# Mixture of experts with 32 experts: the odd ends of two experts in one tile of rows, and the product moved inside SBUF

## The chip, the core and the metric

The kernel runs on one core of a Trainium2 chip. The metric is the device time of one execution in microseconds (us). Engines are named as in the profile: PE is TensorE's matrix multiplication and PEld its weight loads, DVE is VectorE, ACT is ScalarE, POOL is GpSimd, SP is SyncE, which here only issues transfers. "SPq", "ACTq" and "POOLq" are the instruction queues of these engines where they issue transfers or wait. SBUF is the memory on the core (128 partitions), PSUM the accumulator that PE writes, DRAM the large memory.

## What is computed

One decoder layer in float32 on x of 32 x 128 rows of 512: causal differential attention, cross attention with rotary positions, then a mixture of experts, each with a layer norm ahead and a residual. The change is in the last part:

```python
x = hidden_states.reshape(-1, H)                 # 4096 rows of 512
scores = jax.nn.sigmoid(x @ gate_w)              # 32 experts
# two of four groups of experts, then the best TOP_K = 6 experts of each row
sel_flat = selected_experts.ravel()              # 24576 pairs of row and expert
...
g = jax.lax.ragged_dot(xs, w_gate, group_sizes)  # rows sorted by expert; M = 352
u = jax.lax.ragged_dot(xs, w_up, group_sizes)
d = jax.lax.ragged_dot(jax.nn.silu(g) * u, w_down, group_sizes)
...
expert_out = jnp.sum(out * weights[..., None], axis=1)
shared = jax.nn.silu(x @ sw_gate) * (x @ sw_up) @ sw_down
return (expert_out + shared).reshape(B, S, H)
```

How many rows an expert gets depends on the data. Each expert has 2112 KB of weights (w_gate and w_up 704 KB each, w_down 704 KB).

## The kernel before

Self attention comes first, then cross attention with the routing beside it. The class `Routing` writes each pair of row and expert into a table in DRAM (`table_d`), in which every expert has a region of 128 x 32 slots. The shared expert (`Shared.group`) is computed for eight groups of four blocks of rows: three of them (`EARLY = 3`) ahead of the experts, five behind them. Inside the early groups `between()` is called at fixed places and runs the next step of a list `todo`, which brings the routing to its end and prepares the experts.

**Tiles.** `Routing.tiles` (L1036) cuts each expert's region into tiles of 128 rows: an expert with n rows has ceil(n / 128) of them, and the last one is filled in part. `usual` = 4096 x 6 / 128 + 32 / 2 = 208 tiles are always computed, whether used or not; a second loop behind `tc.If(many > usual)` computes the rest, up to 223, if the data need more. `eid` gives each tile's expert, `fresh` whether its weights must be loaded, `rows` its part of the table. Tiles are dealt out in turn to four sets of weights (`SETS = 4`), and each set goes through 52 tiles in the order of the experts, so most tiles find their weights in place. The weights come from SP (`weights_in` L1379, `weights_out` L1400); a load that isn't needed is skipped by its condition.

**Preparation of the tables.** `fetch` (L1309) gathers the tables with POOL, `arrange` and `turn_tables` sort and transpose them on DVE and PE, `places` (L1357) makes from them, for all tiles, the weights (`weight`), the rows to gather (`run_of`) and the rows to add to (`into`). `first_tokens` starts the first three tiles.

**A tile i** goes through these steps, which `run` (L1508) puts in a fixed order on PE, DVE, ACT and POOL (`manual_schedule`):

- `tokens` (L1416): POOL gathers the tile's rows in four indirect transfers (L1422), 128 rows of 512 bytes each, into `e_xr` (three buffers);
- `turn_in`: DVE transposes them (L1434) to `e_xT`;
- `gate_up` (L1439): PE multiplies by `wg` and `wu` (L1447; each float32 matmul shows as two records), ACT takes silu (L1451), DVE multiplies (L1452) into `e_gu`, of which there is one buffer; ACT issues the write of the product to DRAM (L1454);
- `part_out` (L1459): ACT issues the read back from DRAM (L1463) into `e_gr`, with other rows on the partitions, when the write has landed;
- `turn_out`: two transposes on DVE (L1473) to `e_guT`;
- `down` (L1478): PE multiplies by `wd` (L1483), ACT scales into `e_y` (L1487), POOL adds the rows to `sum_d` in DRAM with an indirect transfer that accumulates (L1488).

In iteration i the order is: gate_up(i), turn_in(i+2), turn_out(i-1), weights_in(i+4), down(i-2), weights_out(i+2), part_out(i), tokens(i+5). So POOL's queue holds, in each iteration, the scatter of tile i-2 and then the four gathers of tile i+5.

Behind the experts the five remaining shared groups run, with the same buffers (`s_pool`) as ahead of them, which stay reserved during the experts' loop.

Of the kernel before, what the change touches and what calls it, by code (L numbers as in the profile page):

```python
# [18 lines left out]
P = 128  # L19
# [867 lines left out]
class Routing:  # L887
# [148 lines left out]
    def tiles(self, eid, fresh, rows, used, usual):  # L1036
# [54 lines left out]
        nc.vector.tensor_scalar(n_i, n, float(P - 1), None, ALU.add)  # L1091
        nc.vector.tensor_scalar(n_i, n_i, 7, None, ALU.logical_shift_right)
        nc.vector.tensor_copy(n, n_i)
        end = tile("end", [P, NX])
# [29 lines left out]
        nc.vector.tensor_tensor(fresh, other, first, ALU.max)  # L1124

# [139 lines left out]
class Experts:  # L1265
# [14 lines left out]
    def __init__(  # L1280
        self, cm, ctx, table_ds, h3_d, sum_d, w_gate, w_up, w_down, eid, fresh, rows, n_tiles
    ):
        self.cm, self.h3_d, self.sum_d, self.eid, self.fresh = cm, h3_d, sum_d, eid, fresh
# [9 lines left out]
        self.dram = ctx.enter_context(tc.tile_pool(name="e_dram", bufs=4, space=DRAM))  # L1293
# [7 lines left out]
        self.gu_s = cp.tile([P, self.Q * self.RUN], F32, name="e_gu")  # L1301

# [4 lines left out]
        self.xr, self.xT, self.gu, self.gr, self.guT = {}, {}, {}, {}, {}  # L1307

    def fetch(self):  # L1309
# [17 lines left out]
        nc.gpsimd.memset(self.gu_s, 0.0)  # L1327
# [29 lines left out]
    def places(self):  # L1357

        nc, cp, T, n_tiles = self.cm.nc, self.cp, self.T, self.n_tiles
        entry = self.entry_ps.rearrange("p o j t -> p o (j t)")[:, :, 0:n_tiles]  # L1360
        self.weight = cp.tile([P, n_tiles], F32, name="e_weight")
        nc.vector.tensor_copy(self.weight, entry[:, 1, :])
# [3 lines left out]
        nc.vector.tensor_copy(row, row_i)  # L1366

        self.run_of = cp.tile([P, self.Q, self.NT * P], I32, name="e_run_of")
        nc.vector.tensor_scalar(
            self.run_of, self.parts_ps.rearrange("p t j x -> p t (j x)"), float(self.Q),  # L1370
            float(-self.Q), ALU.mult, ALU.add,
        )
        nc.vector.tensor_scalar(self.run_of, self.run_of, 0.0, row[:, 1:2], ALU.max, ALU.add)
        none = cp.tile([P, n_tiles], F32, name="e_none")
        nc.vector.tensor_scalar(none, entry[:, 0, :], 0.0, row[:, 0:1], ALU.is_equal, ALU.mult)
        self.into = cp.tile([P, n_tiles], I32, name="e_into")
        nc.vector.scalar_tensor_tensor(self.into, entry[:, 0, :], -1.0, none, ALU.add, ALU.add)

    def weights_in(self, i):  # L1379

        if i >= self.end:
            return
# [17 lines left out]
    def weights_out(self, i):  # L1400

        if i >= self.end:
            return
# [12 lines left out]
    def tokens(self, i):  # L1416

        if i >= self.end:
            return
# [10 lines left out]
    def turn_in(self, i):  # L1430
        if i >= self.end:
            return
# [6 lines left out]
    def gate_up(self, i):  # L1439
        if i >= self.end:  # L1440
            return
        nc = self.cm.nc
        pgu = self.cm.banks()
        t, s = self.xT.pop(i), i % SETS
        for half, w in enumerate((self.wg[s], self.wu[s])):
            for c in range(EC):
                nc.tensor.matmul(  # L1447
                    pgu[:, half, 0:M], t[:, c, :], w[:, c, :], start=c == 0, stop=c == EC - 1
                )
        act = self.p2.tile([P, M], F32, name="e_act", bufs=1)  # L1450
        nc.scalar.activation(act, pgu[:, 0, 0:M], AF.Silu)  # L1451
        nc.vector.tensor_tensor(self.gu_s[:, 0:M], act, pgu[:, 1, 0:M], ALU.mult)  # L1452
        self.gu[i] = self.dram.tile([self.Q, P, self.RUN], F32, name="e_gu_d")
        nc.scalar.dma_start(  # L1454
            out=self.gu[i].rearrange("q s m -> s q m"),
            in_=self.gu_s.rearrange("s (q m) -> s q m", q=self.Q),
        )

    def part_out(self, i):  # L1459


        gr = self.gr[i] = self.p2.tile([P, self.Q, self.RUN], F32, name="e_gr")
        self.cm.nc.scalar.dma_start(  # L1463
# [67 lines left out]
def decoder_kernel(  # L1531
# [90 lines left out]
    with tc.manual_schedule(engines=in_order):  # L1622
# [17 lines left out]
        while todo:  # L1640
            between()
# [68 lines left out]
```

## Time and profile before

| | |
|---|---|
| median of 3 runs | 3912.97 us (3909.75 to 3914.64) |
| the profiled execution's own time | 3913.15 us |
| its span | 3911.4 us |
| busy in the span: PE, PEld, DVE, ACT, POOL | 3793.0, 2015.6, 2057.6, 1678.9, 2349.5 us |
| granted TensorE clock | 0.989 of full speed |
| experts' stage, first L1447 to the first L1215 behind it | 2024.05 to 3618.70 us |
| transfers in the span, by queue (POOL, SP, ACT) | 109.85, 190.98, 82.60 MB |

How to read it: a line of the groups gives source line, engine, operation, what is written and read, tile shape and count, then busy time in us and the mean of one in ns, then the engine's idle time just before these instructions with what ended it ("issue": nothing that the profile shows, the engine's own sequencer). A line of a timeline gives start in us, duration in us, engine, line, operation and count, and in brackets the idle time before. Indirect transfers show on POOL with the time in which POOL makes their descriptors; the transfer itself goes on behind that. Matmul ends are modelled, so intervals between starts are more exact than durations.

### The profile page before, as it was taken

To read this page: it belongs to the slowest core of one execution; us is meant where nothing else is said; L and a number is where in the kernel's file an instruction comes from. 1 tells how busy PE (TensorE), PEld (TensorE's weight loads), DVE (VectorE), ACT (ScalarE), POOL (GpSimd) and SP (SyncE) were. 2 spreads that over 40 slices of the span, in tenths; PEclk is the share of its full clock that TensorE was granted. 3 is DMA by queue.
4 is the path that set the end of the run, shared out by engine and by line. 5 is a ranking of instruction groups with operands and counts; after the bars stand their busy time and mean duration, and the time that the engine had idled before them with its cause. 6 is when DMAs were issued, how large, how long until landed. Compare 5 with 4: busy or idle time off the path is not lost. (4 is left out here: it accounts for less than half of the span.)

```text
span 3911.4 us, 58185 instructions
## 1 busy us (share of the span) xinstructions
PE 3793.0 (97%) x19060; PEld 2015.6 (52%) x19060; DVE 2057.6 (53%) x3202; ACT 1678.9 (43%) x4032; POOL 2349.5 (60%) x2582
## 2 busy tenths in 40 slices
PE   8999999899999999999999999999999999999999
PEld 5666666434444444444445555555555555555444
DVE  5888888777877877776133333333333333332111
ACT  6989999757766776666101111111111111111000
POOL 3545545636777777775347777777777777775000
PEclk9999999899999999999999999999999999999999
DMA  3111110121111111111167777767667676766210
GB/s 110 34 34 38 37 34 27 43 87 57 53 60 47 47 47 47 49 47 50 52 178 168 164 166 170 174 151 174 160 153 167 161 170 147 181 151 150 80 64 32
DMA packets 285987, 387.21 MB, mean 99 GB/s; under 512 B 147888, under 2 KB 179248, under 8 KB 285616
## 3 DMA queue, kind: packets, MB, share of 16 engines
q0 software_dynamic: 62912, 109.85, 15.7%
q1 hardware_dynamic: 81792, 190.98, 15.4%
q10 hardware_dynamic: 140976, 82.60, 7.5%
q8 instruction: 154, 2.52, 0.3%
q14 instruction: 153, 1.25, 0.1%
HBM read 617.52 MB, written 143.07 MB: 194 GB/s over the span
## 5 line engine op out<-in xcount | busy, mean ns | idle before, releaser
L1422 POOL DMA_INDIRECT e_xr<-h_d,e_run_of x832 | 849.2, 1021 | 282.1 <-issue 268.1
L695 DVE TENSOR_REDUCE nm<-ps 128x2 f32<-128x1024 f32 x512 | 611.2, 1216 | 112.1 <-PE ps L691 105.3
L1452 DVE TENSOR_TENSOR e_gu<-e_act,ps 128x352 f32<-128x352 f32 x208 | 108.4, 521 | 974.4 <-ACT e_act L1451 548.8
L718 ACT ACTIVATE xp<-ps 128x1024 f32<-128x1024 f32 x512 | 505.9, 1021 | 265.0 <-PE ps L691 200.9
L1483 PE MATMUL ps<-wd,e_guT 128*128 128x512 f32 (+1 forms) x1248 | 585.2, 605 | 34.6 <-ACT e_y L1487 15.7
L714 PE MATMUL ps<-xqn,xk 32*128 32x512 f32 x2048 | 527.1, 620 | 20.6 <-ACT xp L718 19.2
L1447 PE MATMUL ps<-wu,e_xT 128*128 128x352 f32 x1664 | 528.6, 461 | 7.4 <-DMA wu<-in_L_ffn_w_up_dram 5.1
L1447 PE MATMUL ps<-wg,e_xT 128*128 128x352 f32 x1664 | 527.9, 460 | 5.3 <-DMA wg<-in_L_ffn_w_gate_dram 4.5
L691 PE MATMUL ps<-xk,xq 32*128 32x512 f32 x2048 | 526.9, 630 | 0.5 <-DVE nm L695 0.4
L1451 ACT ACTIVATE e_act<-ps 128x352 f32<-128x352 f32 x208 | 96.5, 464 | 935.2 <-PE ps L1447 443.7
L1488 POOL DMA_INDIRECT sum_d<-e_y,e_into x208 | 335.8, 1615 | 178.1 <-ACT e_y L1487 91.6
L1447 PEld LDWEIGHTS ps<-wg,e_xT 128*128 128x128 f32 x1664 | 315.1, 190 | 243.2 <-issue 108.8
L1447 PEld LDWEIGHTS ps<-wu,e_xT 128*128 128x128 f32 x1664 | 316.4, 191 | 186.6 <-DMA wu<-in_L_ffn_w_up_dram 8.3
L279 ACT ACTIVATE s<-s,a_nm 128x128 f32<-128x128 f32 x1024 | 395.7, 396 | 4.9 <-DVE a_nm L265 4.5
L1483 PEld LDWEIGHTS ps<-wd,e_guT 128*128 128x128 f32 (+1 forms) x1248 | 239.8, 194 | 291.7 <-issue 226.5
L1487 ACT ACTIVATE e_y<-ps,e_weight 128x512 f32<-128x512 f32 x208 | 143.0, 687 | 431.3 <-PE ps L1483 265.0
L714 PEld LDWEIGHTS ps<-xqn,xk 32*128 32x128 f32 x2048 | 168.6, 183 | 284.3 <-ACT xp L718 123.3
L1473 DVE STREAM_TRANSPOSE e_guT<-e_gr 96x384 f32<-96x384 f32 (+1 forms) x416 | 230.5, 554 | 76.2 <-DMA e_gr<-e_gu_d 53.5
L228 POOL TENSOR_SCALAR k<-kz,a_keep,a_extra 128x256 f32<-128x256 f32 x128 | 82.6, 655 | 287.4 <-ACT kz L227 287.4
L1028 POOL DMA_INDIRECT table_d<-entry,at x192 | 202.1, 1053 | 64.7 <-issue 53.2
L729 PE MATMUL ps<-xp,v 128*32 128x512 f32 x2048 | 233.0, 595 | 7.9 <-ACT xp L718 7.6
L1434 DVE STREAM_TRANSPOSE e_xT<-e_xr 128x512 f32<-128x512 f32 x208 | 226.3, 1088 | 8.8 <-DMA e_xr<-h_d,e_run_of 8.8
(272 smaller groups left out, 5282.6 us busy)
## 6 DMA issues: line engine op xcount, KB each, us to landing
wg<-in_L_ffn_w_gate_dram SPq DMA_DIRECT2D x208, 704.0 KB
wu<-in_L_ffn_w_up_dram SPq DMA_DIRECT2D x208, 704.0 KB
wd<-in_L_ffn_w_down_dram SPq DMA_DIRECT2D x208, 576.0 KB
e_gu_d<-e_gu ACTq DMA_DIRECT2D x208, 192.0 KB
e_gr<-e_gu_d ACTq DMA_DIRECT2D x208, 192.0 KB
wd<-in_L_ffn_w_down_dram SPq DMA_DIRECT2D x208, 128.0 KB
e_xr<-h_d,e_run_of POOLq DMA_INDIRECT x832
xres<-in_x_dram SPq DMA_DIRECT2D x32, 256.0 KB
```

The source lines that it names most:

```text
L279: nc.scalar.activation(s[:, j, c, side, :], s[:, j, c, side, :], AF.Exp, bias=nm[n][:, side, at : at + 1], accum_out=sm[n][:, to : to + 1],)
L691: self.nc.tensor.matmul(sc[:, i, :], q[rows, ts(c, P)], k[rows, :], start=True, stop=True)
L695: self.nc.vector.tensor_reduce(at[:, self.ROW[side], 2 * pair : 2 * pair + 2], sc, AX.X, ALU.max, negate=True)
L714: self.nc.tensor.matmul(sc[:, i, :], k[rows, ts(c, P)], q[rows, :], start=True, stop=True)
L718: self.nc.scalar.activation(e, sc, AF.Exp)
L729: self.nc.tensor.matmul(po[b, side][ts(j, 32), :], self.v2[b % 2][:, c, 2 * j + side, :], es[j // 2][:, j % 2, :], start=c == 0, stop=c == ...
L1422: self.cm.nc.gpsimd.indirect_dma_start(out=xr[:, t, :], out_offset=None, in_=self.h3_d.rearrange("t (q f) -> (t q) f", q=self.Q), in_offse ...
L1434: self.cm.nc.vector.transpose(xT.rearrange("p c (t i) -> p c t i", t=self.Q), self.xr.pop(i).rearrange("p t (j c) -> p c t j", c=EC),)
L1447: nc.tensor.matmul(pgu[:, half, 0:M], t[:, c, :], w[:, c, :], start=c == 0, stop=c == EC - 1)
L1473: self.cm.nc.vector.transpose(t[rows, 0:n, :].rearrange("p c (t i) -> p c t i", t=self.Q), g[rows, :, 0 : 32 * n].rearrange("p t (j c) -> ...
L1483: nc.tensor.matmul(py, t[:n, c, :], self.wd[s][:n, c, :], start=c == 0, stop=c == len(M_CHUNKS) - 1)
L1488: nc.gpsimd.indirect_dma_start(out=self.sum_d[:, :], out_offset=bass.IndirectOffsetOnAxis(ap=self.into[:, i : i + 1], axis=0), in_=y[:, :] ...
```

## The change

There are now 192 whole tiles (`usual`) and 8 shared ones (`mixed`). `Routing.tiles` counts each expert's rows in units of 64. If that number is odd, the last 64 slots are an odd end; the first 16 odd ends go two by two into shared tiles, and further ones get a tile of their own as before. The threshold of the second loop is now 192 of 223 tiles.

- `Routing.halves` (new) works out on DVE, by comparing and summing, which expert and which rows of the table belong to each of the 16 ends.
- `fetch_halves`, `arrange_halves`, `turn_halves`, `places_of_halves`, `mixed_places` (new) do for the ends what the steps above do for tiles. They stand in `todo` behind `first_tokens`: four table gathers on POOL, sorting on DVE, six small transposes on PE in the last early shared group, and small DVE instructions.
- `mixed_loads` (new): the weights of the two experts of a shared tile don't come from SP but are gathered by POOL, row by row: ten indirect transfers for each shared tile, four with rows of 5632 bytes (704 KB each) and six with rows of 2048 bytes. One is issued at the end of each of the first ten iterations, and again of the ten iterations behind each shared tile. There is one buffer for each of the two experts (`xg`, `xu`, `xd`).
- `seq` places shared tile m at position 25 m + 14 of 200.
- In a shared tile, PE multiplies the lower 64 columns by one expert's weights and the upper 64 by the other's, alternately, into the two halves of the same PSUM tile.
- A shared tile is added to `sum_d` in two scatters, one for each half; in each, the other half's rows go to unused rows. Both halves may hold the same row of x.
- The product stays in SBUF: `part_out` and the DRAM buffers are gone, there are two `e_gu` buffers, and ACT issues four transfers of 48 KB (eight of 24 KB in a shared tile) from `e_gu` to `e_gr`.
- `e_gu`, `e_gr`, the scaled result (`e_out`, four buffers, before `e_y` with two) and the shared tiles' weights lie in a pool of their own, made in the room of the shared groups' buffers and of cross attention's; the shared groups' buffers are made again behind the experts.

The diff, cut to its core:

```diff
@@ Routing.tiles
-        nc.vector.tensor_scalar(n_i, n, float(P - 1), None, ALU.add)
-        nc.vector.tensor_scalar(n_i, n_i, 7, None, ALU.logical_shift_right)
+        nc.vector.tensor_scalar(n_i, n, float(P // 2 - 1), None, ALU.add)
+        nc.vector.tensor_scalar(n_i, n_i, 6, None, ALU.logical_shift_right)
+        odd_i = tile("odd_i", [P, NX], I32)
+        nc.vector.tensor_scalar(odd_i, n_i, 1, None, ALU.bitwise_and)
...
+        nc.vector.tensor_scalar(alone, nth, float(2 * mixed), None, ALU.is_le)
+        nc.vector.tensor_tensor(odd, odd, alone, ALU.mult)
+        nc.vector.tensor_tensor(n, n, odd, ALU.subtract)
@@ Experts
+    def mixed_loads(self):
+        top = (self.Q - 1) * 32
+        rows = [w.rearrange("e (p c) m -> (e p) (c m)", p=P) for w in self.w_in]
+        out = self.w_out.rearrange("e k m -> (e k) m")
+        for m in range(self.mixed):
+            work = [
+                (x[h].rearrange("p c m -> p (c m)"), src, P, 0, h)
+                for x, src in zip((self.xg, self.xu), rows) for h in range(2)
+            ] + [
+                (self.xd[h][:, c, :], out, top if c == 2 else P, 1 + c, h)
+                for c in range(len(M_CHUNKS)) for h in range(2)
+            ]
+            for to, src, n, at, h in work:
+                k = 2 * m + h
+                self.cm.nc.gpsimd.indirect_dma_start(
+                    out=to[0:n],
+                    out_offset=None,
+                    in_=src,
+                    in_offset=bass.IndirectOffsetOnAxis(ap=self.x_rows[0:n, at, k : k + 1], axis=0),
+                    bounds_check=src.shape[0] - 1,
+                )
+                yield
@@ gate_up
+            for half, w in enumerate((self.xg, self.xu)):
+                for c in range(EC):
+                    for h in range(2):
+                        lanes = ts(h, P // 2)
+                        nc.tensor.matmul(
+                            pgu[lanes, half, 0:M], t[:, c, lanes], w[h][:, c, :],
+                            start=c == 0, stop=c == EC - 1,
+                        )
...
-        nc.scalar.dma_start(
-            out=self.gu[i].rearrange("q s m -> s q m"),
-            in_=self.gu_s.rearrange("s (q m) -> s q m", q=self.Q),
-        )
-    def part_out(self, i):
...
+        for q in range(self.Q):
+            to, part = gr[ts(q, 32)], gu[:, ts(q, self.RUN)]
+            if i < self.n_tiles:
+                nc.scalar.dma_start(out=to, in_=part)
+            else:
+                for h in range(2):
+                    nc.scalar.dma_start(out=to[:, ts(h, 2), :], in_=part[ts(h, P // 2)])
@@ down
+        for into in [self.into[:, i : i + 1]] if m < 0 else [self.into_half[:, h, m : m + 1] for h in range(2)]:
+            nc.gpsimd.indirect_dma_start(
+                out=self.sum_d[:, :],
+                out_offset=bass.IndirectOffsetOnAxis(ap=into, axis=0),
...
+                compute_op=ALU.add,
+            )
@@ run
+            for k in range(len(seq) + 2):
+                each(self.gate_up, k)
+                each(self.turn_in, k + 2)
+                each(self.turn_out, k - 1)
+                each(lambda i: self.weights_in(i + SETS), k)
+                each(self.down, k - 2)
...
+                each(self.tokens, k + 5)
+                if left:
+                    next(loads, None)
+                    left -= 1
+                if k < len(seq) and seq[k] >= self.n_tiles:
+                    left = 10
@@ decoder_kernel
-    usual = T * TOPK // P + NX // 2
+    usual, mixed = T * TOPK // P, NX // 4
...
             experts.first_tokens,
+            experts.fetch_halves,
+            nothing,
+            nothing,
+            experts.arrange_halves,
+            experts.turn_halves,
+            experts.places_of_halves,
+            experts.mixed_places,
         ]
...
+    x_out.close()
+    e_out = ExitStack()
+    experts.rooms(e_out.enter_context(tc.tile_pool(name="e_p3", bufs=1, reuse_waits="tile")))
     experts.run()
```

## The prediction

> **What bounds the kernel now.** I read the table of busy time by stage first, because the change touches one stage only, the expert stage. Columns: stretch in us, its length, then busy us and count of PE, PEld, DVE, ACT and POOL, the granted clock, the DMA share and GB/s.
>
> ```profile
> 2024.00:3619.00 1595.00, 1546.26 (x4579) 871.61 (x4578) 535.94 (x831) 238.96 (x416) 1163.24 (x1019) 0.99 0.69 162
> ```
>
> PE is busy for 97% of the stage and POOL for 73%, so PE looks like the only bound. The groups of POOL's instructions in the same stage correct this: each indirect transfer has idle time in front of it that ends by "issue", that is, by nothing but POOL's own sequencer.
>
> ```profile
> L1422 POOL DMA_INDIRECT e_xr<-h_d,e_run_of x812 | 828.9, 1021 | 255.6 <-issue 241.9 <-DVE e_xT L1434 10.0 <-DVE e_gu L1452 3.4
> L1488 POOL DMA_INDIRECT sum_d<-e_y,e_into x208 | 335.8, 1615 | 178.1 <-ACT e_y L1487 91.6 <-issue 72.9 <-DMA sum_d<-e_y,e_into 13.5
> ```
>
> The timelines of the two engines over the same 10 us show what that means for a tile (start, duration, instruction):
>
> ```profile
> 2065.78 1.61 POOL L1488 DMA_INDIRECT sum_d<-e_y,e_into  x1 [0.30 <-issue]
> 2067.70 1.06 POOL L1422 DMA_INDIRECT e_xr<-h_d,e_run_of  x1 [0.30 <-issue]
> 2069.06 1.00 POOL L1422 DMA_INDIRECT e_xr<-h_d,e_run_of  x1 [0.31 <-issue]
> 2070.37 1.01 POOL L1422 DMA_INDIRECT e_xr<-h_d,e_run_of  x1 [0.30 <-issue]
> 2071.68 1.01 POOL L1422 DMA_INDIRECT e_xr<-h_d,e_run_of  x1 [0.30 <-issue]
> 2073.00 1.62 POOL L1488 DMA_INDIRECT sum_d<-e_y,e_into  x1 [0.30 <-issue]
> ```
>
> ```profile
> 2062.87 2.53 PE L1447 MATMUL ps<-wg,e_xT 128*128 128x352 f32 x8
> 2065.24 2.53 PE L1447 MATMUL ps<-wu,e_xT 128*128 128x352 f32 x8
> 2067.61 2.74 PE L1483 MATMUL ps<-wd,e_guT 128*128 128x512 f32 x6
> 2070.18 2.53 PE L1447 MATMUL ps<-wg,e_xT 128*128 128x352 f32 x8
> ```
>
> A tile costs PE 2070.18 - 2062.87 = **7.31 us**, and POOL 2073.00 - 2065.78 = **7.22 us** (four gathers 5.30, one scatter 1.92). POOL is within 1.2% of PE: nothing can be put on it without making it the bound. The stage lasts from 2024.05 (first L1447) to 3618.70 (first L1215 behind it), 1594.65 us. 208 x 7.31 = 1520.5; the other 74 are about 17 for the last tiles' chain and 57 of PE waits, with matmuls at half pace behind a long one:
>
> ```profile
> 3573.17 5.46 PE L1483 MATMUL ps<-wd,e_guT 128*128 128x512 f32 x6 [4.09 <-DVE e_guT L1473]
> ```
>
> (six records took 5.46 us, otherwise 2.74). In that time POOL waited too: from its first gather for the sixth tile (2031.39) to its last (3578.4 + 1.0) are 1548 us, with 203 x 5.30 + 201 x 1.92 = 1462 of work and some 86 of waiting, mostly the 91.6 behind e_y.
>
> **The change, part by part.** *Tiles on PE.* From the reference's inputs the experts receive 673 to 842 rows; in units of 64 rows that makes 191 whole tiles and exactly 16 odd ends. So 192 + 8 tiles do, and the loop for more than 192 is skipped. PE saves 8 x 7.31 = 58.5 us. A shared tile has twice the records, each on 64 columns of the array; two neighbours should run together. No row has 64 columns; 32 columns, four at a time, is the nearest:
>
> ```profile
> 1305.02 3.64 PE L729 MATMUL ps<-xp,v 128*32 128x512 f32 x32 [0.25 <-ACT xp L718]
> 1305.48 0.13 PEld L729 LDWEIGHTS ps<-xp,v 128*32 128x32 f32 x4 [0.30 <-issue]
> 1305.90 0.13 PEld L729 LDWEIGHTS ps<-xp,v 128*32 128x32 f32 x4 [0.30 <-issue]
> ```
>
> Four records go every 0.43 us, the pace of one full one (2.57 us for six of L1483), and their weights load beside them. Each change of array shape costs about 0.2 (L1254's four records fill 1.06 us, 2022.99 to 2024.05, instead of 0.86), four changes per shared tile: 8.1 us each, +6 in all; if nothing overlapped, +58. I take +6: PE work 1468 us. The Trainium skill, "TensorE: Matmul & The Clock Gate", Part 3, speaks against that: a weight load overlaps a running matmul only if its row group differs, and both halves use all 128 rows. L729's loads use the same rows too and start with the matmuls of the round before, so the trace decides; by the rule, with 22 pairs of loads exposed at 0.11 to 0.19 us, a shared tile would take 10 to 11 us as an estimate, some 20 us in all.
>
> *POOL.* From the same point (first gather of the sixth tile) to the last gather there are now:
> - gathers for 195 tiles: 195 x 5.30 = 1033.5;
> - scatters in between: 193 tiles, of which 8 scatter twice: 201 x 1.92 = 386;
> - 80 weight gathers (10 per shared tile). The trace has none with rows of 5632 or 2048 bytes. Gathers of 512-byte rows take 1.01, the table's (L1320) of 1 KB 1.01 to 1.09, scatters of 8 bytes (L1028) 0.97: length does not show. The other end is the accumulating scatter with 2 KB rows, 1.61. With 0.30 in front: 80 x 1.27 = 102 to 80 x 1.91 = 153. I take 80 x 1.31 = 105, the row that also gathers;
> - a wait in each pair of scatters: POOL holds a scatter until the one before has landed (the third releaser of L1488 above). By the trace's landing events a scatter lands 4.9 us after its start (median of 202, longest 9.3), so the second starts 3.0 later than it could. In seven of eight a 704 KB gather is issued just ahead in the same queue (such a load from SP lands in 4.5). I take 4 each, 32; ends 0 and 8 x 7.4 = 59.
>
> Sum 1556.5. Behind the waiting scatter stand the next tile's four gathers, for which DVE and then PE wait.
>
> *Start.* POOL issues the ends' table gathers behind the first 12 token gathers (1997.50 + 12 x 1.31 = 2013.2), 5.2 us with four; they land near 2020, DVE sorts them in about 1.5, and PE's six small transposes, which stand in its order at about 2018.5, wait: +3.5 for all that follows. Ends: 0, and 6 if the 38 small DVE instructions (0.16 to 0.25 each, some 8 us) also make the table transposes at 1987.69 late; the tables were sorted at 1985.5, 2.2 us earlier. The 20 gathers ahead of the loop end 6.4 us later than before, inside POOL's idle 7.87 before 2031.39.
>
> *Product within SBUF.* One hop replaces two, and no instruction on ACT waits any longer for the write to DRAM. ACT issues four transfers for two, 4 x 0.37 instead of 0.71 us, at 239 busy us of 1595. This can remove up to the 57 us of PE waits; I count 0, since POOL is then late instead. The cover gone (POOL cheap), it counts. The Trainium skill, "DMA: Bandwidth & Descriptors", Rules for kernel authors, has transfers under 64 KB as mostly overhead, and these are 48 KB; with the 2.0 us of fixed cost that its section on the anatomy of one DMA gives for GpSimd's path, four one after another would be, as an estimate, 8 us for a tile, over PE's 7.31. No run here shows SBUF to SBUF; the 192 KB reads took 2.4 us to land at the median.
>
> *DMA and the end.* The bounce took 18.3% of the engines' time in the stage (79.5 MB); the weight gathers bring 16 x 2.16 = 35 MB, at the rate of SP's weights (67 MB in 13.5%) 7%. The share falls, so I count 0. At the end s_gu and its pool are laid out again over the experts' tiles; they are needed 7 us into the group, when the last scatter has landed: 0.
>
> *Sum.* Last gather ends at 2031.4 + 3.5 + 1556.5 = 3591.4. Behind it come landing 2.1 (3.1 from its start), transpose 1.1, gate and up 4.7, down of the tile before the last but one 2.6, and two more downs with the last product's way, about 6: 16.5. The shared groups start at 3608 instead of 3618.7: -10.8, and 1.8 I give back for waits that a queue at its limit will meet: -9. The profiled execution took 3913.15 (span 3911.4), 0.2 above the median of the runs, 3912.97. Forecast **3904**.
>
> **The rivals.** *PE stays the bound*: POOL's additions fit in after all. Then start 3.5 + 1468 + 57 + 17 = 1545.5, -49: 3864; 3807 if the waits go too. For it: POOL idled 86 us. Against it: these idle times were PE's stalls, and 105 + 32 us of new work are more. *A weight gather costs what an accumulating scatter costs*: long rows make POOL write more descriptors. Then 80 x 0.60 = 48 more, 3952, slower; it decides from 1.31 + 9/80 = 1.42 us for a gather with its gap. For it: the only 2 KB rows of the trace take 1.61; against it: those accumulate, and 8 to 1024 bytes cost alike. *It does not do what it says*: counts differ on the chip, more than 192 whole tiles, and the second loop runs its 31: +227, 4131.
>
> **How the numbers follow.** POOL the bound at its rows: 0.60, from 3885 (pairs at 2 us, start at 0) to 3922 (pairs at 6, start at 6); of that 0.34 faster, 0.20 within, 0.06 slower. PE the bound 0.10 (faster). Dear gathers 0.27 (slower). Second loop 0.03 (slower). A difference under 0.2% (8 us) can't be told from none. Range 3872 to 3950: it leaves out the second loop, half of "PE the bound" and a third of the dear gathers, 0.17.
>
> **What would show it.** POOL in the expert stage without idle time other than "issue", DVE's e_xT waiting for e_xr, and PE idle before the gate matmuls (L1621 in the changed kernel) for DVE: right. POOL waiting for e_y as now: wrong, PE is the bound. The weight gathers' mean against 1.01, the idle time before the second scatter against 4, a shared tile's PE time against 8.1, the first L1621 against 2028, and the waits of PE for e_guT, which should go, test the terms one by one.

## The result and the profile after

The changed kernel takes 4089.44 us (median of 4 runs, 4063.41 to 4107.61), the kernel before on the same chip 3911.36: a ratio of **1.045 (1.039 to 1.0509)**, slower. The forecast was 3904, the range ended at 3950. The profiled execution of the changed kernel took 4107.61, its span 4105.9.

The expert stage of the changed kernel, in the columns of the table by stage above (stretch, length, busy us and count of PE, PEld, DVE, ACT, POOL, granted clock, DMA share, GB/s):

```profile
2024.00:3830.00 1806.00, 1574.42 (x4618) 854.38 (x4617) 514.74 (x820) 226.85 (x402) 1215.91 (x1072) 0.94 0.61 141
```

The stage begins as before (first L1621 at 2024.2) and now ends at 3809.96 (first L1268; the last 20 us of the stretch are the shared groups'), 191 us later. PE is busy for 87% of it, POOL for 67%: both shares fell (from 97% and 73%), so waiting has grown on both. Its groups show who waits:

```profile
L1599 POOL DMA_INDIRECT e_xr<-h_d,e_run_of x800 | 817.4, 1022 | 271.8 <-issue 229.7
L1664 PE MATMUL ps<-wd,e_guT 128*128 128x512 f32 (+1 forms) x1152 | 600.0, 661 | 220.9 <-issue 144.6
...
L1671 POOL DMA_INDIRECT sum_d<-e_out,e_into x192 | 310.3, 1616 | 259.9 <-ACT e_out L1668 186.8
L1668 ACT ACTIVATE e_out<-ps,e_weight 128x512 f32<-128x512 f32 x200 | 137.4, 687 | 774.9 <-DMA e_gr<-e_gu 300.0
```

800 gathers are 200 tiles, so the second loop did not run. PE stands before `down` for 221 us (34.6 before), POOL before its scatter for 260 us (178 before), mostly for ACT's e_out, as it did for e_y. Two different things lie in this, and one loading iteration shows both. First POOL's timeline in the changed kernel (start, duration, instruction, idle time before):

```profile
2871.16 1.61 POOL L1671 DMA_INDIRECT sum_d<-e_out,e_into  x1 [0.30 <-issue]
2873.07 1.06 POOL L1599 DMA_INDIRECT e_xr<-h_d,e_run_of  x1 [0.30 <-issue]
2874.44 1.01 POOL L1599 DMA_INDIRECT e_xr<-h_d,e_run_of  x1 [0.31 <-issue]
2875.76 1.01 POOL L1599 DMA_INDIRECT e_xr<-h_d,e_run_of  x1 [0.31 <-issue]
2877.07 1.01 POOL L1599 DMA_INDIRECT e_xr<-h_d,e_run_of  x1 [0.30 <-issue]
2878.39 1.01 POOL L1538 DMA_INDIRECT xu<-in_L_ffn_w_up_dram,e_x_rows  x1 [0.30 <-issue]
2879.70 1.61 POOL L1671 DMA_INDIRECT sum_d<-e_out,e_into  x1 [0.30 <-issue]
...
2904.03 1.01 POOL L1538 DMA_INDIRECT xd<-in_L_ffn_w_down_dram,e_x_rows  x1 [0.30 <-issue]
2911.40 1.61 POOL L1671 DMA_INDIRECT sum_d<-e_out,e_into  x1 [6.36 <-ACT e_out L1668]
```

An iteration with a weight gather takes POOL 8.54 us (2871.16 to 2879.70) without any pause, where PE needs 7.31: POOL is the bound there. That I had forecast. The second thing I had not. PE and ACT in the same stretch:

```profile
2876.74 2.53 PE L1621 MATMUL ps<-wu,e_xT 128*128 128x352 f32 x8
2879.11 2.74 PE L1664 MATMUL ps<-wd,e_guT 128*128 128x512 f32 x6
2881.68 2.53 PE L1621 MATMUL ps<-wg,e_xT 128*128 128x352 f32 x8
2884.05 2.53 PE L1621 MATMUL ps<-wu,e_xT 128*128 128x352 f32 x8
2894.06 4.72 PE L1664 MATMUL ps<-wd,e_guT 128*128 128x512 f32 x6 [7.47 <-issue]
```

```profile
2877.04 0.69 ACT L1668 ACTIVATE e_out<-ps,e_weight 128x512 f32<-128x512 f32 x1 [3.23 <-remote]
2890.91 0.46 ACT L1634 ACTIVATE e_act<-ps 128x352 f32<-128x352 f32 x1 [13.19 <-remote]
2891.96 2.52 ACTq L1641 DMA_DIRECT2D e_gr<-e_gu  x4
...
2906.77 0.46 ACT L1634 ACTIVATE e_act<-ps 128x352 f32<-128x352 f32 x1 [10.84 <-remote]
```

PE has done the `wu` matmuls by 2879.3, ACT has been free since 2877.7, and yet the silu that needs nothing else starts at 2890.91, **11.6 us late**. The view names "remote" as its releaser, that is, no instruction that it can tell, and the trace records PE's signal at 2890.83: the signal itself arrived late. DVE's signal to PE does not: `wd` at 2894.06 starts 0.1 us after the transpose that it waits for. This goes on for one more tile, until POOL, out of work, pauses from 2905.04 to 2911.40; 1.7 us into this pause four of PE's signals are recorded within 0.26 us, and ACT goes on at 2906.77. PE has meanwhile waited 7.47 us, and its next six records take 4.72 us instead of 2.74.

The kernel before has it too. ACT's waits for such signals, before and then after (engine, tile, line, releaser: us, times, longest):

```profile
ACT e_act L1451 <- remote: 153.6, 24, 10.8
```

```profile
ACT e_act L1634 <- remote: 296.6, 35, 13.2
```

The 4.09 us of PE's waiting at 3573.17, which I had shown in the prediction, are of this kind, though the view gives "PE" as the releaser: PE's `wu` ended at 3561.8, silu began at 3570.03, 1.2 us after POOL had stopped at 3568.81 (PE, POOL and ACT of the kernel before):

```profile
3559.24 2.53 PE L1447 MATMUL ps<-wu,e_xT 128*128 128x352 f32 x8
3567.80 1.01 POOL L1422 DMA_INDIRECT e_xr<-h_d,e_run_of  x1 [0.30 <-issue]
3570.03 0.46 ACT L1451 ACTIVATE e_act<-ps 128x352 f32<-128x352 f32 x1 [9.51 <-PE ps L1447]
```

### The profile page after: what moved, and what is told of

Same layout as the page of the kernel before. It is cut to its first block, busy times and chain, and to the rows that moved or that the text cites. A ratio compares the mean times of both kernels' runs of the same rounds, so it can differ in the third digit from the quotient of the medians.

```text
span 4105.9 us, 58585 instructions
## 1 busy us (share of the span) xinstructions
PE 3804.0 (93%) x19066; PEld 1989.4 (48%) x19066; DVE 2042.8 (50%) x3231; ACT 1664.8 (41%) x4016; POOL 2402.4 (59%) x2638
## 3 DMA queue, kind: packets, MB, share of 16 engines
q8 instruction: 154, 2.52, 0.3%
## 5 line engine op out<-in xcount | busy, mean ns | idle before, releaser
L1599 POOL DMA_INDIRECT e_xr<-h_d,e_run_of x800 | 817.4, 1022 | 271.8 <-issue 229.7
L1664 PE MATMUL ps<-wd,e_guT 128*128 128x512 f32 (+1 forms) x1152 | 600.0, 661 | 220.9 <-issue 144.6
L1621 PE MATMUL ps<-wg,e_xT 128*128 128x352 f32 x1536 | 488.4, 460 | 3.2 <-DMA wg<-in_L_ffn_w_gate_dram 2.0
L1621 PE MATMUL ps<-wu,e_xT 128*128 128x352 f32 x1536 | 486.9, 459 | 3.1 <-issue 3.0
L1671 POOL DMA_INDIRECT sum_d<-e_out,e_into x192 | 310.3, 1616 | 259.9 <-ACT e_out L1668 186.8
L1668 ACT ACTIVATE e_out<-ps,e_weight 128x512 f32<-128x512 f32 x200 | 137.4, 687 | 774.9 <-DMA e_gr<-e_gu 300.0
L1621 PEld LDWEIGHTS ps<-wg,e_xT 128*128 128x128 f32 x1536 | 292.3, 191 | 230.0 <-issue 105.1
L1621 PEld LDWEIGHTS ps<-wu,e_xT 128*128 128x128 f32 x1536 | 291.7, 190 | 166.0 <-issue 4.0
L1651 DVE STREAM_TRANSPOSE e_guT<-e_gr 96x384 f32<-96x384 f32 (+1 forms) x400 | 219.5, 549 | 46.1 <-DMA e_gr<-e_gu 26.6
L1609 DVE STREAM_TRANSPOSE e_xT<-e_xr 128x512 f32<-128x512 f32 x200 | 217.3, 1086 | 35.6 <-DMA e_xr<-h_d,e_run_of 35.5
```

Of the source, the lines that this page charges most:

```text
L1599: self.cm.nc.gpsimd.indirect_dma_start(out=xr[:, t, :], out_offset=None, in_=self.h3_d.rearrange("t (q f) -> (t q) f", q=self.Q), in_offse ...
L1609: self.cm.nc.vector.transpose(xT.rearrange("p c (t i) -> p c t i", t=self.Q), self.xr.pop(i).rearrange("p t (j c) -> p c t j", c=EC),)
L1621: nc.tensor.matmul(pgu[:, half, 0:M], t[:, c, :], w[:, c, :], start=c == 0, stop=c == EC - 1)
L1651: self.cm.nc.vector.transpose(t[rows, 0:n, :].rearrange("p c (t i) -> p c t i", t=self.Q), g[rows, :, 0 : 32 * n].rearrange("p t (j c) -> ...
L1664: nc.tensor.matmul(py[lanes], t[:n, c, lanes], wd[:n, c, :], start=c == 0, stop=c == last)
L1671: nc.gpsimd.indirect_dma_start(out=self.sum_d[:, :], out_offset=bass.IndirectOffsetOnAxis(ap=into, axis=0), in_=y[:, :], in_offset=None, b ...
```

## The experiments

My theory after this result: POOL is the bound where it gathers weights, and on top of it PE's signals come late while POOL issues without pause. Rivals: the transfers within SBUF slow ACT or the loads; the weight gathers cost by the traffic they bring, not by POOL's time; the pair of scatters is the price.

The chips differ. The kernel before takes 3911 to 3914 us where the result and e1 to e4 were taken, and 3854 on the three chips of all other runs, so each ratio is against the kernel before on the same chip.

| run | us | before | ratio (95%) |
|---|---|---|---|
| e1_loads_once | 3978.46 | 3913.71 | 1.0148 (1.011 to 1.0187) |
| e2_dram_path | 4041.17 | 3913.71 | 1.0316 (1.0295 to 1.0336) |
| e3_sbuf_only | 3954.10 | 3913.71 | 1.0092 (1.0071 to 1.0113) |
| e4_gathers_only | 4024.12 | 3913.71 | 1.0274 (1.0249 to 1.0298) |
| e5_sp_loads | 3907.96 | 3853.56 | 1.0146 (1.0126 to 1.0166) |
| e6_act_order | 3855.58 | 3853.56 | 1.0011 (1.0000 to 1.0022) |
| e7_pool_busy | 3944.79 | 3853.56 | 1.0227 (1.021 to 1.0244) |
| e8_three_gathers | 3855.04 | 3853.56 | 1.0004 (0.9995 to 1.0014) |
| e9_after | 3946.50 | 3853.94 | 1.0244 (1.0224 to 1.0263) |
| e3b_sbuf_only | 3855.29 | 3853.94 | 1.0009 (0.9998 to 1.0019) |
| e10_sp_loads_order | 3885.50 | 3853.94 | 1.0078 (1.0061 to 1.0095) |
| e11_sp_loads_dram | 3895.94 | 3853.94 | 1.0102 (1.0084 to 1.012) |
| e4b_gathers_only | 3964.77 | 3853.86 | 1.0291 (1.0273 to 1.0308) |
| e12_one_load | 3844.35 | 3853.86 | 0.9975 (0.9966 to 0.9985) |
| e13_spread | 3881.13 | 3853.86 | 1.0075 (1.0058 to 1.0093) |
| e14_one_scatter | 3811.76 | 3853.86 | 0.9887 (0.9871 to 0.9904) |
| e15_late_scatter_dram | 3881.76 | 3854.40 | 1.0074 (1.0059 to 1.0088) |
| e16_late_scatter_sbuf | 3869.61 | 3854.40 | 1.0043 (1.003 to 1.0057) |

### The parts one by one

**e1_loads_once**: the changed kernel; weights are gathered for the first shared tile alone.

```diff
-        for m in range(self.mixed):
+        for m in range(1):
             work = [
```

> The changed kernel, but POOL gathers the shared tiles' weights only for the first of the eight; the other seven multiply by those of the first, so their rows are wrong and 70 of 80 weight gathers are left out. Theory A (POOL's queue: while POOL makes descriptors for indirect transfers with no pause over 1 us, PE's signals that its matmuls are done reach ACT late; the weight gathers remove POOL's pauses): a tile costs POOL 7.22 us again against PE's 7.31, the late signals fall back to what they are in the kernel before (214 us in sum on ACT against 462), and the time is 3860 to 3910 us. Theory B (the four transfers inside SBUF: 2.5 us of issue on ACT for a tile, and their completion semaphores shared with SP's weight loads): only 70 x 1.31 us can go, 4000 us or more. Theory C (the shared tiles themselves, their matmuls on half the columns and their second scatter): 4000 us or more.

**e2_dram_path**: the changed kernel with the product through DRAM, as before.

```diff
-        for q in range(self.Q):
-            to, part = gr[ts(q, 32)], gu[:, ts(q, self.RUN)]
...
+        d = self.gu[i] = self.dram.tile([self.Q, P, self.RUN], F32, name="e_gu_d")
+        if i < self.n_tiles:
+            nc.scalar.dma_start(
+                out=d.rearrange("q s m -> s q m"), in_=gu.rearrange("s (q m) -> s q m", q=self.Q)
+            )
...
+                each(self.part_out, k)
                 each(self.tokens, k + 5)
```

> The changed kernel with the product by way of DRAM as before (one write and one read on ACT for a tile, eight writes and one read for a shared tile). Theory A (weight gathers keep POOL without pauses): little changes, 4050 to 4110 us. Theory B (four transfers inside SBUF): back to 3905 to 3930 us. Theory C (shared tiles): as A.

**e3_sbuf_only**: 208 whole tiles as before, the product within SBUF. **e4_gathers_only**: 208 whole tiles, the product through DRAM, and the 80 weight gathers into buffers that nobody reads.

```diff
-    usual, mixed = T * TOPK // P, NX // 4
+    usual, mixed = T * TOPK // P + NX // 2, NX // 4
...
-            lambda: routing.tiles(eid, fresh, rows, used, usual, mixed),
+            lambda: routing.tiles(eid, fresh, rows, used, usual, 0),
...
-        experts.begin(0, usual, mixed)
+        experts.begin(0, usual)
```

> Only the second half of the change: 208 whole tiles and no shared ones, no weight gathers, the product moved inside SBUF by four transfers. Theory A: POOL has the work of the kernel before, so 3890 to 3915 us. Theory B: the four transfers are the cause and the time is 4000 us or more. Theory C: as A.

> 208 whole tiles with the product by way of DRAM, as in the kernel before, and 80 weight gathers on POOL in eight groups of ten iterations, into buffers that nothing reads. Theory A: 4030 us or more: the ten iterations of each group cost POOL 8.53 us instead of 7.22, and in them PE's signals come late as in the changed kernel. Theories B and C: only POOL's sum counts, 80 x 1.31 = 105 us less the some 86 us that POOL waits in the kernel before, about 3932 us.

Against the kernel before, the changed kernel has +178 us, e1 +65, e2 +127, e3 +40, e4 +110. The gathers are worth some 110 by both ways of asking: e1 leaves 70 of the 80 out (178 - 65 = 113), e4 adds them. The way within SBUF costs 40 by itself and 178 - 127 = 51 in the changed kernel, where I had counted nothing or a gain. e1, e2 and e3 each fall between the ranges set for the theories, so no single theory is the whole cause; e4 comes 6 us under what the first one asked for.

### What a gather costs by

**e7_pool_busy**: e4 with a POOL instruction of about the same length, without traffic, in place of each weight gather. **e8_three_gathers**: whole tiles through DRAM with three of four token gathers; DVE copies the third quarter for the fourth. **e5_sp_loads**: the changed kernel, the shared tiles' weights loaded by SP. **e6_act_order**: e3 with ACT's four transfers behind the e_out of the same iteration.

```diff
@@ e7
-                self.cm.nc.gpsimd.indirect_dma_start(
...
+                self.cm.nc.gpsimd.memset(self.xg[0].rearrange("p c m -> p (c m)")[:, 0:1408], 0.0)
@@ e8
-        for t in range(self.Q):
+        for t in range(self.Q - 1):
...
+        nc.vector.tensor_copy(xr[:, 3, :], xr[:, 2, :])
@@ e5
+                for to, src in zip((self.xg[h], self.xu[h]), self.w_in):
+                    e = expert(2 * m + h)
+                    self.last = nc.sync.dma_start(
+                        out=to, in_=src[ds(e, 1)].rearrange("o (p c) m -> p (o c) m", p=P)
+                    )
+                    yield
@@ e6
                 each(self.down, k - 2)
+                each(self.part_out, k)
```

> The changed kernel, but SP loads the shared tiles' weights (eight plain transfers for each tile, spread over six iterations) and POOL gathers none. Theory A (the weight gathers cost by POOL's queue): as the run in which they were left out, or a little less, 3955 to 3985 us, though as many bytes move. Rival A' (the 35 MB of weights cost by the DMA engines, whoever issues them): 4050 us or more.

> 208 whole tiles with the product moved inside SBUF, as in the run that took 3954 us, but ACT issues the four transfers of tile k behind e_out of tile k-2 and not ahead of it. Theory A, second part (each time that POOL runs dry, it waits until ACT has done e_act, issued the transfers, 2.5 us, and done e_out): POOL's pauses become about 2 us shorter and the time falls to 3890 to 3915 us. Rival B' (the transfers cost by the semaphores that they share with SP's weight loads, or by their own number): 3945 us or more.

> 208 whole tiles with the product by way of DRAM, as in the run with 80 weight gathers that nothing reads (4024 us), but each of these gathers is replaced by a memset of 128x1408 on POOL, which should take about 1.2 us like a gather with its gap. Theory A, first part (it is the making of descriptors without a pause that holds PE's signals back): the memsets are pauses in it, the signals come in time, and the time is 3945 us or less. Rival A'' (any work that fills POOL does the same, since POOL's own chain of scatter and gathers is the bound in these iterations): 4005 to 4035 us.

> 208 whole tiles with the product by way of DRAM, as in the kernel before, but POOL gathers only three quarters of each tile's rows (the fourth is a copy of the third on DVE, so the experts' output is wrong): POOL has 5.9 us of work for a tile and pauses in each. Theory A: PE's signals come in time and the 57 us of PE's waits go: 3850 to 3865 us. Rival (the late signals have another cause, PE's own queue or the weight loads): 3900 us or more.

The group of POOL's added instructions in e7:

```profile
L1540 POOL MEMSET xg<- 128x1408 f32 x80 | 103.3, 1291 | 0.0
```

103 us of POOL's time without a byte moved cost 91. **A gather costs mostly by POOL's time**: on such a chip the real gathers, 80 x 1.31 = 105 us of it, cost 111 (e4b below). The 20 us between the two can be traffic, for PE's waits for weights are 20.8 us in e4b and 6.8 in e7; they were not taken apart. But e8 gives POOL 1.31 us less in each tile and gains nothing: in the kernel before, on this chip, PE alone is the bound. POOL at 7.22 beside PE's 7.31 is harmless; at 8.54 nearly all of the excess counts. With the weights by SP (e5) POOL is relieved, 38 us quicker than the changed kernel on such a chip (e9 below), but PE now waits for whole tiles' weights: 40.5 us for `wd` and 27.9 for `wg`. e6's order changes nothing here (3855.58; e3b, without it, 3855.29).

This chip's kernel before was 60 us quicker than the first one's, and no ACT row with "remote" was in these traces. The expectations of these four stand in the first chip's times; without late signals e6, e7 and e8 do not test what they say of such signals. So the changed kernel itself had to be run on such a chip.

### The changed kernel on another chip

**e9_after** is the changed kernel, unchanged; **e3b_sbuf_only** repeats e3. **e10_sp_loads_order** is e5 with e6's order, **e11_sp_loads_dram** e5 with the product through DRAM.

```diff
@@ e10: e5, and
                 each(self.down, k - 2)
+                each(self.part_out, k)
@@ e11: e5, and
+        nc.scalar.dma_start(
+            out=d.rearrange("q s m -> s q m"), in_=gu.rearrange("s (q m) -> s q m", q=self.Q)
+        )
```

> The changed kernel itself, beside the kernel before on the same chip, because the kernel before took 3913 us on one chip and 3854 us on another, where PE's signals were never late. If PE's late signals make most of the loss, the changed kernel loses little on a chip without them (under 2%); if POOL's queue and SP's late weight loads make it, it loses 3 to 4.5% on any chip.

> 208 whole tiles with the product moved inside SBUF, transfers ahead of e_out, once more, beside the kernel before on the same chip. If the transfers' 2.5 us on ACT cost only by making the pauses longer that follow PE's late signals: within 0.3% of the kernel before on a chip without late signals, 1% slower on one with them. If they cost by themselves: 1% slower on any chip.

> Shared tiles with their weights loaded by SP, and the four (eight) transfers inside SBUF issued behind e_out. In the run with SP's loads and the old order (1.0146 of before), PE waited 80 us for wg and wd, whose loads SP issued late: it waited 270 us in front of wg and wu for product transfers that shared their completion semaphores. That theory (eight semaphores for eight transfers in an iteration): still 1.01 or more of before. Rival (what is late is e_out, and by it POOL and all that follows): below before, 0.99.

> Shared tiles with their weights loaded by SP, and the product by way of DRAM as before (one write, one read; two reads in a shared tile), so that an iteration uses six completion semaphores and not eight. Theory of the semaphores: SP is no longer late, the 8 x 7.31 - 6 = 52 us of PE come through for the most part, 0.988 to 0.993 of before. Rival (a shared tile's second scatter and its other steps cost what it saves): 1.00 or more.

The same program takes 3946.5 here and 4089.4 there: 143 us that go with the chip, and all of them lie in the experts' stage (the first L1621 stands at 2024.2 there and 2024.4 here, and behind the stage come 296 and 294 us). The ratio of e9 lies between its two forecasts, under 2% and 3 to 4.5%. Of the way within SBUF nothing is left (e3b 1.0009). e10 and e11 stay over the kernel before: PE waits 37.1 us for `wg` and 16.6 for `wd` in e10; 25.2, 16.7 and 14.4 for `wg`, `wu` and `wd` in e11. e11 speaks against the theory that completion semaphores (the signals that a transfer has landed) shared by too many transfers make the weights late: it forecast 0.988 to 0.993. e10 fits neither of its two. A loading iteration of e9, PE and then ACT:

```profile
2592.53 2.53 PE L1621 MATMUL ps<-wu,e_xT 128*128 128x352 f32 x8
2594.90 2.74 PE L1664 MATMUL ps<-wd,e_guT 128*128 128x512 f32 x6
```

```profile
2591.53 0.69 ACT L1668 ACTIVATE e_out<-ps,e_weight 128x512 f32<-128x512 f32 x1 [3.23 <-DMA e_gr<-e_gu]
2595.16 0.46 ACT L1634 ACTIVATE e_act<-ps 128x352 f32<-128x352 f32 x1 [2.94 <-PE ps L1621]
2596.21 2.52 ACTq L1641 DMA_DIRECT2D e_gr<-e_gu  x4
```

Silu starts 0.1 us after the last `wu` record, with POOL as busy as on the other chip. I summed, for each trace, the time by which silu and e_out started over 0.9 us after ACT was free and PE's modelled end was past: 214 us in the kernel before, 462 after, 314 in e1, some 390 to 400 in e2, 306 in e3, 410 in e4; on the chips where the kernel before takes 3854, not one such event. Where there are such events, they gather in stretches in which POOL issues with no pause over 0.9 us. In the kernel before 32 such stretches, 18 to 51 us long, hold all 78 events: 55 of the late starts come while POOL still issues, the other 23 at most 1.2 us into its next pause. In the changed kernel the stretches are 7 to 68 us long and the pause reaches 1.8 us. On the other chips POOL runs 135 us (e9) and 217 us (e4b) without a pause and nothing comes late.

### The rest of the price

**e4b_gathers_only** repeats e4 here. **e12_one_load**: e11, the weights loaded for the first shared tile alone. **e13_spread**: e11 with a load in every third iteration. **e14_one_scatter**: e12 with the first of the two scatters alone.

```diff
@@ e12
-        for m in range(self.mixed):
+        for m in range(1):
@@ e13
-                    if left <= 6:
+                    if left % 3 == 0 or k < 14:
                         next(loads, None)
...
-                    left = 8
+                    left = 20
@@ e14
-        for into in [self.into[:, i : i + 1]] if m < 0 else [self.into_half[:, h, m : m + 1] for h in range(2)]:
+        for into in [self.into[:, i : i + 1]] if m < 0 else [self.into_half[:, 0, m : m + 1]]:
```

> 208 whole tiles, product by way of DRAM, 80 weight gathers that nothing reads, once more, beside the kernel before on the same chip. On a chip where PE's signals are not late (before at 3854 us) the same with memsets in place of the gathers took 91 us more than before. If the gathers cost by the time that they take in POOL's order, the same here: 85 to 100 us. If most of their 111 us on the first chip came from late signals: under 60 us.

> Shared tiles, product by way of DRAM, SP loads the shared tiles' weights only for the first of the eight (the others multiply by these, so their rows are wrong). If the 66 us that PE waits for weights in the run with all eight (42 us over before) come from these loads, in SP's queue or on the DMA engines: 0.988 to 0.994 of before. If they come from the order in which SP's other loads stand around a shared tile, or from the second scatter: 1.005 or more.

> As the run with shared tiles, SP's loads and the product by way of DRAM (1.0102 of before), but the loads of a shared tile stand in every third iteration and not in six iterations one after another. If it is their crowding: below 1.000 of before. If it is their number, or another cause: 1.005 or more.

> As the run with SP's loads for the first shared tile only, and each shared tile is added with its first scatter alone (the rows of its second half are left out). If the second scatter's wait (4 us each, 29.7 to 37.5 us in eight, in the traces) is on the path: 25 to 45 us below that run. If POOL's pauses hide it: within 8 us of it.

e4b costs 111, as e4 did (110), where 85 to 100 or under 60 were expected: the gathers' price does not depend on late signals. e11 against e12 is 52 us: seven shared tiles' weights by SP, which then come late; spread out (e13) they still cost 37. e14 against e12 is 33 us: the second scatters, on the path. e12 and e14 are quicker than the kernel before, but only without a part of the work; e14's -42 is what fewer tiles bring when only the first shared tile's loads stand against it.

**e15_late_scatter_dram** and **e16_late_scatter_sbuf** issue the second scatter behind the next tile's gathers, so that it need not wait, on e13 and on e10 with e13's spread loads.

```diff
-        for into in [self.into[:, i : i + 1]] if m < 0 else [self.into_half[:, h, m : m + 1] for h in range(2)]:
...
+            self.add(y, self.into_half[:, 0, m : m + 1])
+            self.later = y, self.into_half[:, 1, m : m + 1]
...
                 each(self.tokens, k + 5)
+                if mixed[1]:
+                    self.add(*self.later)
```

> The version that the runs point to: shared tiles, their weights loaded by SP in every third iteration, the product by way of DRAM, and the second scatter of a shared tile issued behind the next tile's four gathers (5.3 us), by when the first has landed (4.9 us). The run with spread loads took 1.0075 of before, the second scatter's wait 33 us: 3881 - 33 = 3848, 0.997 to 1.000 of before. If the wait only moves to another place: 1.005 or more.

> The same with the product inside SBUF, its transfers issued behind e_out: 79 MB less on the DMA engines, so that the weights land earlier, against eight completion semaphores in an iteration. With six loads crowded it took 1.0078 of before where DRAM took 1.0102. If the DMA engines' load makes the weights late: 0.990 to 0.996 of before. If the semaphores do: 1.000 or more.

POOL's waits before its scatter in e13, then in e15:

```profile
POOL sum_d L1694 <- DMA sum_d<-e_out,e_into: 36.5, 21, 4.1
POOL sum_d L1694 <- DMA sum_d<-e_out,e_into_half: 32.0, 8, 6.3
```

```profile
POOL sum_d L1700 <- DMA sum_d<-e_out,e_into: 50.8, 22, 4.1
...
POOL sum_d L1700 <- DMA sum_d<-e_out,e_into_half: 5.4, 3, 4.2
```

e15 gains nothing (1.0074 against 1.0075). The wait only moved: the eight plain scatters that now stand right behind a late one waited 33.5 us in all, whatever the view names as their releaser, where the pairs of e13 had waited 32.0. e16 is the quickest version with shared tiles and the whole output, still 15 us over the kernel before: none here beats it. Its 1.0043 falls on the side of the semaphores, which e11 spoke against. PE waits 12.2 us for `wg` and `wu` in e16 and 45.7 in e15 (whose profiled execution, 3901 us, is the slowest of its six); the two differ in the product's way and in ACT's order, and what makes the weights late stays open.

## Why the prediction was wrong, point by point

**What failed.** The step "*Product within SBUF* ... This can remove up to the 57 us of PE waits; I count 0, since POOL is then late instead" is the largest miss. I took the 57 us for waits that a later POOL would cover. They were PE's signals coming late on this chip while POOL does not pause, and a late signal holds POOL too: its scatter waits for e_out, 186.8 us in the row L1671 of the profile after (5.8 in e9), for which the sum had nothing. My sign that PE is the bound, POOL waiting for the scaled result, thus showed where neither engine was. Taken as the difference between the chips, the late signals cost 59 us in the kernel before (3913 - 3854) and 143 after. More work on POOL does not raise this price by itself: the gathers alone leave it at 59 (e4 - e4b: 4024.1 - 3964.8), though silu and e_out then start late by 410 us in sum and not 214. The way within SBUF alone turns 59 into 99 (e3 - e3b: 3954.1 - 3855.3), and the whole change makes it 143. So the way within SBUF is what costs on this chip, and more so with the rest of the change. How it does so is my reading of the chain, not a test: when POOL pauses, a delayed silu, the product, ACT's transfers and e_out must run before the next scatter, and ACT's issue of four transfers takes 2.52 us ahead of e_out (row L1641), where I had 4 x 0.37 = 1.48 and the kernel before 0.37.

**The other 42 us** remain on a chip without late signals (3946 against 3904). The step is "*Sum*", its "1.8 I give back for waits that a queue at its limit will meet". In e9 POOL's intervals from scatter to scatter are 7.42 us on average in the 114 plain iterations and 8.70 in the 71 with one load, for 7.22 and 8.53 by my rows: 23 + 12 = **35 us**, not 1.8. POOL's waits of e9 tell where:

```profile
POOL sum_d L1671 <- issue: 77.2, 168, 5.0
POOL sum_d L1671 <- DMA sum_d<-e_out,e_into_half: 33.5, 8, 5.2
POOL sum_d L1671 <- DMA sum_d<-e_out,e_into: 29.2, 15, 4.0
```

The last row is a wait that I had charged to the pairs alone: 15 plain scatters waited for the one before them to land, 29 us, all but one of them ahead of the last gather. Some 11 us more are long waits that end by "issue". It is not PE's slower pace: 98 of the 114 plain intervals take under 7.25 us, POOL's own pace, and the excess lies in the few others. Why those scatters landed late stays open. So the last gather ended at 3623.7, 32 later than the 3591.4 of the sum (35, less 3 for the start), and what follows took 25.9 us instead of 16.5: the last tile's gate starts 8.9 us after its last gather (3632.63), where I had 3.2 for landing and transpose, because PE, without a pause since 3573.60, was still busy with the tile before (POOL, then PE, of e9):

```profile
3622.70 1.01 POOL L1599 DMA_INDIRECT e_xr<-h_d,e_run_of  x1 [0.30 <-issue]
```

```profile
3632.63 2.53 PE L1621 MATMUL ps<-wg,e_xT 128*128 128x352 f32 x8
...
3649.64 5.10 PE L1268 MATMUL ps<-s_hT,sg 128*128 128x512 f32 x8 [3.42 <-ACTq L1857]
```

**What held.** Second loop not run. *Weight gathers*: 80 at 1.00 to 1.01 us and 0.30 in front, as taken; their length of row does not show, and the dear-gather rival is out. *The pair's wait*: 33.5 / 8 = 4.2 us in e9 and 37.5 / 8 = 4.7 after, for 4, and it is on the path (e14). *Start*: I gave it 3.5 us; it cost next to nothing: the first L1621 stands at 2024.2, and the sixth tile's first gather in e9 at 2031.8, for 2031.4 before. *A shared tile on PE*: the records of e9 around one, its `xg`, `xu` and `xd` between those of whole tiles:

```profile
2328.26 2.59 PE L1629 MATMUL ps<-xg,e_xT 128*64 128x352 f32 x16
2330.67 2.54 PE L1629 MATMUL ps<-xu,e_xT 128*64 128x352 f32 x16
2333.14 2.85 PE L1664 MATMUL ps<-wd,e_guT 128*128 128x512 f32 x6
2335.82 2.53 PE L1621 MATMUL ps<-wg,e_xT 128*128 128x352 f32 x8
...
2347.96 2.80 PE L1664 MATMUL ps<-xd,e_guT 128*64 128x512 f32 x12
2350.69 2.63 PE L1621 MATMUL ps<-wg,e_xT 128*128 128x352 f32 x8
```

Sixteen half records take 2.41 to 2.47 us from start to start, eight whole ones 2.37: neighbours on the two column halves run together. The three groups of a shared tile take 7.61 us, and the changes of shape add 0.39 to the groups of whole tiles beside them: 8.0 us, the same for all eight, where I had 8.1. The rule of the Trainium skill ("TensorE: Matmul & The Clock Gate", Part 3) that I had weighed, a weight load hidden only under another row group, would have given 10 to 11 us as an estimate; the trace does not show it. The estimate of 8 us for four transfers, from the page "DMA: Bandwidth & Descriptors", is not shown either: e9 issues four transfers every 7.31 us (from 2596.21, then 2603.52), and DVE's 400 e_guT transposes stand idle for 8.5 us in its whole stage.

The account of a chip without late signals: eight tiles fewer -58.5 + 8 x 0.69 = -53 (worked out), second scatters +33, gathers +111, way within SBUF +1 (measured): +92, where the whole change measures +92.6. The run nearest to the first term is e14, -42 with one shared tile's loads by SP still in it; that the sum comes so close is in part luck. On a chip with late signals the four are -53, +33, +110, +40: +130 of the measured +178. The other 48 came when all parts ran together, and were not taken apart.

**Open.** Why PE's signals come late on some chips and not on others. That POOL's issuing without pause brings it about is a coincidence in time in the traces that have it, not a test: no kernel with added pauses was run on such a chip. Nor was e6's order run on one, which takes the 2.5 us of issuing off the way to the scatter. That the difference between the chips is all made by late signals was not tested either; I know of no other difference in the traces.

## What to carry to other kernels

Where two engines are within a per cent or two of each other, nearly all work added to the second is paid: 103 us of memsets on POOL cost 91, where POOL had 0.09 us to spare in a tile. A wait that ends by "remote" or "issue" while the named producer has long been done is no slack that other work may use; find out first what ends it, and whether it is there on another chip. Before saving work on the bound engine, price what carries the saving: here 53 us on PE were bought with 33 for the second scatters and 111 for the gathers.

## What the runs showed of the hardware

- Where the kernel before takes 3911 to 3914 us, PE's signals reached ACT up to 11.6 us late in stretches in which POOL issued without a pause over 0.9 us (18 to 51 us long in the kernel before). The same program took 59 us (before), 99 (e3) or 143 (after) more there than on the three other chips, whose traces have no such event. The cause is open.
- ACT spends 0.55 to 0.61 us on issuing each transfer of 48 KB from SBUF to SBUF (2.52 us for four), 0.37 on one of 192 KB to DRAM.
- SP's weight loads waited for the product's transfers to land: up to 24.3 us in the changed kernel (23.6 in e9), where the longest of the kernel before (`e_gr<-e_gu_d`) is 6.2. The number of transfers alone does not make it: with the same four for each of 208 whole tiles (e3b) the longest is 8.1. SP's own waits in the changed kernel:

```profile
SPq L1587 <- DMA e_gr<-e_gu: 121.4, 21, 14.6
SPq L1575 <- DMA e_gr<-e_gu: 80.8, 26, 24.3
```

- A POOL gather costs the same 1.01 us whether its 128 rows have 512 or 5632 bytes.
